# Four graph-attention layers over 128 graphs: rehearsed due times, layer 1's fold on another engine, and a repeat of rows without DRAM for two graphs

## The chip, the cores and the metric

The kernel runs on one core of one Trainium2 chip. The metric is the device time of one launch in microseconds, median over runs. A core has five engines, each with its own instruction stream executed in order: TensorE (PE; matmuls and transposes, with its weight loads shown as PEld), VectorE (DVE), ScalarE (ACT), GpSimd (POOL) and SyncE (SP, which here only issues DMA transfers). They wait for each other by semaphores. PE's results land in PSUM, eight banks of 128 x 512 floats.

## The reference

Input are 128 graphs of 128 nodes with 512 features each (float32), and an adjacency matrix per graph. For each graph four graph-attention layers follow each other, each adding to the residual stream `x`:

```
h = relu(layernorm(x))
layer 0: Wh = h @ W^T;  e = leaky_relu(Wh@a1 + (Wh@a2)^T), masked;  x += elu(softmax(e) @ h)
layer 1: xl = h @ W1 (512 -> 4 heads x 256); per head a score from xl.a_src and xl.a_dst,
         masked softmax over sources, out = attn^T @ xl, + bias, elu;
         then one head: gl = out @ W2 (1024 -> 512), same attention; x += result + bias
layer 2: scores from h.w_src and h.w_dst;  x += softmax(masked leaky_relu) @ h
layer 3: 8 heads x 64: Wh = h @ Wp; score from a 128-vector per head; x += relu(attn @ Wh)
```

A score of the form (h @ W) . a equals h . (W @ a), for layer 0 with W^T. The kernel uses this: products of the weights with the attention vectors ("folds") are made once, and stand as extra columns beside the weights (`w1x`, `w2x`, `wpx`) or as a row `u1`, `u2` on all partitions.

## The kernel before, in words

**Streams.** Each graph's work is a Python generator, `graph(b)`, that yields steps: one instruction, or a `Group` of up to four matmuls or transposes. It also yields requests: `Take` (a buffer of a tag with a fixed number of buffers), `Fork` (a second stream beside this one), `Join` (wait for that stream), `Until` (wait for a name, such as `"w1"`, to be reached). Ten graphs (`FLYING`) are in flight. When one ends, the next is started. Each graph forks the load of the graph two later (`AHEAD`).

**The order of issue.** `Scheduler.issue` builds the program once, at build time: among the next steps of all streams it takes the smallest (earliest start by estimated durations, rank, age). So the order within each engine's queue is fixed, and an instruction waits behind those that were put before it. `rank` of a graph's step is age x pace + due, where due comes from `plan`: the position of that step in the list of graph 0's steps, spread over the time of ten graphs. `plan` runs in `advance` when the first graph has ended. Until then `due` is None and all ranks are 0. Streams that aren't graphs (loads, the set-up, forks) always have rank 0.

**Set-up.** `setup()` is one stream of age 0.5. It issues the 4-byte-piece loads of `a1`, `a2`, `b1` on SP, then all weights in pieces of 512 KB to 1 MB on SP's queue, among them four attention vectors broadcast to all partitions (512 KB each for layer 1, 256 KB each for layer 2's), then two times four matmuls for `u1` and `u2` on PE; then `fold`, one DVE product-and-sum per column: 32 of 256 elements for layer 1's four heads, four row blocks and two vectors, then 16 of 512 for W2, then 16 DVE operations for Wp.

**The layers.** `norm_relu`: bn_stats and small steps on DVE and POOL, then h on ACT. `transposed`: PE transposes into a bank, ACT copies out. `projected`: matmul groups of four over the row blocks of a weight, ACT copies out. Layer 1 has 3 x 4 matmuls of 344 columns (w1x), 8 of 128 (et,xl), and 2 x 8 of 257 (w2x); layer 3 has 2 x 4 of 264 (wpx) and 8 of 65 (x,sd). In layers 0, 1 (its second half) and 2 the score row is repeated over the partitions by a PE transpose of a broadcast column (`attended`).

**`spread`** does the same for several rows: 4 rows of layer 1, 16 and later 8 of layer 3. One PE transpose, ACT writes `r`, SP writes `r` to DRAM (`d`), and SP reads it back broadcast to all partitions. Layer 1's spread and layer 3's second one are forks; layer 3's first one is part of the graph's stream. In layer 3 `sd` (1 MB, tag with 2 buffers) receives the 16 rows; DVE adds the mask, takes the maximum per row; the 8 rows of maxima are spread again; ACT applies Prelu and exp, PE multiplies (x,sd).

**Buffers that matter.** bank 8; `sd` 2; `x3` (layer 3's projection, filled from wpx and read by x,sd) 2; `ht` 3; `r4`, `r8`, `r16` 3 each; `junk` (the unused elementwise output of a dot) 2.

In the profile every graph instruction bears line L237, the call in `issue` (L245 in the changed kernel), so groups are told apart by their tiles: "bank<-w2x,y" is a matmul of weights `w2x` and `y` into a bank.

Of the kernel before, what the change touches and what calls it, by code (L numbers as in the profile page):

```python
# [22 lines left out]
AHEAD = 2  # L23

# [78 lines left out]
class Fork:  # L103


    def __init__(self, steps):
        self.steps = steps
# [21 lines left out]
class Scheduler:  # L129
    def __init__(self):  # L130
        self.streams = []
        self.engine_free = {}
        self.written = {}
        self.moved = 0.0
        self.taken = {}
        self.returned = {}
        self.tag_of = {}
        self.last_use = {}
        self.reached = set()
        self.done = []  # L140
        self.pace = 0.0
        self.due = None

    def give_back(self, *aps):
        for ap in aps:
            name = ap.tensor.name
            tag = self.tag_of.pop(name)
            self.taken[tag] -= 1
            heapq.heappush(self.returned[tag], self.last_use.get(name, 0.0))
# [7 lines left out]
    def advance(self, s):  # L157

        while True:
            want = s.next  # L160
            if want is None:
                try:
# [3 lines left out]
                    if s.like and self.due is None:  # L166
                        self.plan()
# [5 lines left out]
            if isinstance(want, Take):  # L173
                back = self.returned.setdefault(want.tag, [0.0] * want.bufs)
                if not back:
                    return
                self.taken[want.tag] = self.taken.get(want.tag, 0) + 1
                t = want.pool.tile(
                    want.shape, want.dtype, tag=want.tag, name=want.tag, bufs=want.bufs
                )  # L180
                self.tag_of[t.tensor.name] = want.tag
                self.written[t.tensor.name] = heapq.heappop(back)
                s.answer = t
            elif isinstance(want, Fork):
                s.answer = self.add(want.steps, s.age)
# [7 lines left out]
    def plan(self):  # L193

        load, length, self.due = {}, 0.0, []
        for step in self.done:
            self.due.append(length)
            load[step.engine] = load.get(step.engine, 0.0) + step.busy
            length += step.busy + step.delay
# [3 lines left out]
    def rank(self, s):  # L203
        if not s.like:
            return 0.0
        if not self.due:
            return 0.0
# [12 lines left out]
    def issue(self):  # L220
# [13 lines left out]
        if s.like and self.due is None and s.age == 0:  # L234
            self.done.append(step)
# [29 lines left out]
def kernel(  # L265
# [65 lines left out]
    nc.vector.tensor_scalar(off_diag, ident, -1.0, 1.0, ALU.mult, ALU.add)  # L331
    minus_half = const.tile([P, 1], F32, name="minus_half")
# [6 lines left out]
    w1x = const.tile([P, KC, E1 + HF], F32, name="w1x")  # L339
    w1 = w1x[:, :, E1:]  # L340
    w2x = const.tile([P, FC, E2 + D], F32, name="w2x")
    w2 = w2x[:, :, E2:]
    wpx = const.tile([P, KC, H3, E3 + K3], F32, name="wpx")
    wp = wpx[:, :, :, E3:]
# [10 lines left out]

    def on_all_partitions(t, row):
        return S.dma_start(out=t, in_=row.partition_broadcast(P))

    def fold(weight, vec, n, to):

        junk = yield tile_of("junk", 2, D)
        yield V.tensor_tensor_reduce(
            out=junk[:, :n],
            in0=weight,
            in1=vec,
            scale=1.0,
            scalar=0.0,
            op0=ALU.mult,  # L370
            op1=ALU.add,
            accum_out=to,
        )
        give_back(junk)

    def setup():
        acs = []
        for a in (l0_a1, l0_a2):
            acs.append(const.tile([P, KC], F32, name=f"ac{len(acs)}"))
            with nc.allow_non_contiguous_dma(reason="512 values, once"):  # L380
                nc.sync.dma_start(out=acs[-1], in_=a.rearrange("(c p) o -> p (c o)", p=P))
        with nc.allow_non_contiguous_dma(reason="1024 values, once"):
            nc.sync.dma_start(out=b1, in_=l1_b1.rearrange("(c p) -> p c", p=P))
# [3 lines left out]
        yield S.dma_start(out=w0, in_=l0_w.rearrange("(c p) f -> p c f", p=P))  # L387
        abs1 = []
        for a in (l1_src1, l1_dst1):
            ab = yield tile_of("y1", 2, FC, P)  # L390
            abs1.append(ab.rearrange("p c q -> p (c q)"))
            yield on_all_partitions(abs1[-1], a.rearrange("h f -> (h f)"))
        for c in range(0, KC, 2):
            yield S.dma_start(
                out=w1[:, c : c + 2, :],
                in_=l1_w1[c * P : (c + 2) * P].rearrange("(c p) f -> p c f", p=P),
            )
        abs2 = []
        for i, a in enumerate((l1_src2, l1_dst2)):
            abs2.append((yield tile_of("x2", 2, E2 + D))[:, :D])  # L400
            yield on_all_partitions(abs2[-1], a[0])
        for c in range(0, FC, 4):
            yield S.dma_start(
                out=w2[:, c : c + 4, :],
                in_=l1_w2[c * P : (c + 4) * P].rearrange("(c p) f -> p c f", p=P),
            )
        yield on_all_partitions(b2, l1_b2)
        yield on_all_partitions(w_src, l2_src)
        yield on_all_partitions(w_dst, l2_dst)
        yield on_all_partitions(b_l2, l2_b)  # L410
        yield S.dma_start(out=b_l3[:, 0], in_=l3_batt.partition_broadcast(P))
        wab = yield tile_of("sd", 2, 2 * H3, P)
        wa = wab.rearrange("p s q -> p (s q)")[:, : H3 * 2 * K3]
        yield on_all_partitions(wa, l3_watt.rearrange("h k -> (h k)"))
        wa = wa.rearrange("p (h k) -> p h k", h=H3)
        for c in range(KC):
            yield S.dma_start(
                out=wp[:, c], in_=l3_wp[c * P : (c + 1) * P].rearrange("p (h k) -> p h k", h=H3)
            )
        for ac, u in zip(acs, (u1, u2)):  # L420
            pu = yield bank()
            for c in range(KC):
                yield T.matmul(
                    pu,
                    lhsT=ac[:, c : c + 1].to_broadcast([P, P]),
# [4 lines left out]
            yield A.copy(u, pu)  # L430
            give_back(pu)
        give_back(w0)
        sched.reached.add("u")
        for c in range(KC):
            for s, ab in enumerate(abs1):
                for h in range(H1):
                    f = slice(h * F1, (h + 1) * F1)
                    to = w1x[:, c, s * H1 + h : s * H1 + h + 1]
                    yield from fold(w1[:, c, f], ab[:, f], F1, to)
        give_back(*abs1)  # L440
        sched.reached.add("w1")
        for c in range(FC):
            for s, ab in enumerate(abs2):
                yield from fold(w2[:, c, :], ab, D, w2x[:, c, s : s + 1])
        give_back(*abs2)
        sched.reached.add("w2")
        for c in range(KC):
            for s in range(2):
                prod = yield tile_of("junk", 2, D)
                p3 = prod.rearrange("p (h k) -> p h k", h=H3)  # L450
                yield V.tensor_tensor(p3, wp[:, c], wa[:, :, s * K3 : (s + 1) * K3], ALU.mult)

                yield V.tensor_reduce(wpx[:, c, :, 1 - s], p3, AX.X, ALU.add)
                give_back(prod)
        give_back(wab)
# [19 lines left out]
    def dot(h, vec, to):  # L475

        yield from fold(h, vec, D, to)

    def transposed(t, n, tag, bufs):

        r = yield tile_of(tag, bufs, n, P)
        pt = yield bank()
        yield Group(
            [T.transpose(pt[:, j * P : (j + 1) * P], t[:, j, :], ident) for j in range(n)]
# [5 lines left out]
    def spread(cols, n, to, func):  # L490


        r = yield Take(work, [n, P], f"r{n}", 3)
# [62 lines left out]
    def attended(own, other, mask, values, exact=False):  # L556
# [5 lines left out]
        et = yield from transposed(e, 1, "et0", 3)  # L562
# [6 lines left out]
    def projected(lhs, n_k, w, parts, to, beside=None):  # L569


        width = w.shape[2] // parts
        fork = None
        for i in range(parts):
            lo = i * width
            pm = yield bank()
            for g in range(0, n_k, 4):
# [5 lines left out]
                            rhs=w[:, c, lo : lo + width],  # L583
# [38 lines left out]
    def layer1(xt, mask):  # L622
        h = yield from norm_relu(xt)
        yield G.tensor_tensor(xt, xt, b2, ALU.add)
        ht = yield from transposed(h.rearrange("p (c q) -> p c q", q=P), KC, "ht", 3)
# [6 lines left out]
            ht, KC, w1x, 3, columns(fx, 3), lambda: spread(fx[:, :H1], H1, rows, AF.Copy)  # L632
# [6 lines left out]
        et = yield from transposed(e, H1, "et1", 3)  # L639
# [52 lines left out]
    def layer3(xt, mask, mask_t):  # L692
# [3 lines left out]
        ht = yield from transposed(h.rearrange("p (c q) -> p c q", q=P), KC, "ht", 3)  # L696
# [3 lines left out]
        fx = yield tile_of("x3", 2, H3, E3 + K3 + 1)  # L700
# [5 lines left out]
            wpx.rearrange("p c h k -> p c (h k)"),  # L706
# [7 lines left out]
        yield from spread(  # L714
            f.rearrange("p s h -> p (s h)"), 2 * H3, sd.rearrange("p s q -> p (s q)"), AF.Copy
        )
        d, e = sd[:, :H3], sd[:, H3:]
# [7 lines left out]
        fork = yield Fork(spread(mx, H3, d.rearrange("p h q -> p (h q)"), AF.Prelu))  # L725
# [44 lines left out]
    def load(b):  # L770

        if b % AG == 0:
# [4 lines left out]
        xs[b] = xpool.tile([P, D], F32, tag="xt", name="xt")  # L777
        yield S.dma_start(out=xs[b], in_=x[b])
# [7 lines left out]
    def graph(b):  # L786
        if b + AHEAD < B:
# [16 lines left out]
        yield from layer1(xt, m1)  # L804
# [7 lines left out]
        yield from layer3(xt, m3, m3t)  # L812
# [4 lines left out]
    with tc.manual_schedule():  # L817
        for i in range(min(AHEAD, B)):
            sched.add(load(i), i)
        flying = [sched.add(graph(0), 0, "graph")]  # L820
# [58 lines left out]
```

## Time and profile before

| | us |
|---|---|
| median of 3 runs | 3452.57 (3451.44 to 3454.29) |
| profiled execution | 3451.47 |
| its span, first to last instruction | 3449.7 |
| PE / DVE / ACT / POOL busy | 3362.5 / 2882.3 / 2379.8 / 1022.3 |
| w2x matmuls (4096 records, two to a matmul) | 975.0 busy |
| w1x matmuls (3072) | 953.5 |
| wpx matmuls (2048) | 499.6 |
| first matmul / first w1x / first w2x starts at | 11.83 / 43.64 / 78.53 |
| last h,et matmul (last graph, layer 2) starts at | 3391.58 |
| DMA moved, mean over the span | 94 GB/s |

How to read it: busy time is the sum over an engine's instructions. In the slices each digit is the busy share of a fortieth of the span (86 us) in tenths; PEclk is the clock granted to PE, in tenths of full. A line of the timeline gives the start (us from the span's start), the time covered, the engine, the line, the operation with its tiles, the size and the count, and in brackets the idle time before it and what ended it. A line of the view by stages gives the stretch, its length, the busy time of PE, PEld, DVE, ACT and POOL (instructions in brackets), the granted clock, the busy share of the DMA engines and GB/s. An idle stretch of an engine that isn't the bound costs nothing.

### The profile page before, as it was taken

What the parts mean: (1) busy time and instruction counts of PE and PEld (TensorE: products, weight loads), DVE (VectorE), ACT (ScalarE), POOL (GpSimd) and SP (SyncE); (2) the same over time, 40 slices, a digit from 0 to 9 for tenths busy, and PEclk for the clock granted to TensorE, in tenths of its full rate; (3) what the DMA queues carried; (4) which work ended last, traced back from release to release, by engine and by line L of the source; (5) the groups of instructions that cost most, each with busy time, mean ns of one, the idle gap of its engine ahead of it and who ended that gap; (6) DMA issues with size and microseconds to landing.
All of it is one profiled execution on the core that took longest, in us unless ns stands there. A gap on an engine that the chain in (4) does not pass through costs nothing.

```text
span 3449.7 us, 55292 instructions
## 1 busy us (share of the span) xinstructions
PE 3362.5 (97%) x16912; PEld 2619.4 (76%) x16912; DVE 2882.3 (84%) x9330; ACT 2379.8 (69%) x6659; POOL 1022.3 (30%) x1800
## 2 busy tenths in 40 slices
PE   5899999999999999999999999999999999999995
PEld 3677777777777777777777777777777777777774
DVE  7778888888888888888888888888888888888875
ACT  3567776777777777777777777777777777777763
POOL 2323233233233233233233233233233233233210
PEclk7999999999999999999999999999999999999996
DMA  4112222222222222222222222222222222222222
GB/s 159 38 56 102 98 85 102 98 87 102 97 86 102 96 90 102 94 89 102 93 92 101 92 91 101 92 95 100 91 93 99 92 96 99 90 95 99 84 89 99
DMA packets 126346, 325.00 MB, mean 94 GB/s; under 512 B 21088, under 2 KB 41056, under 8 KB 109664
## 3 DMA queue, kind: packets, MB, share of 16 engines
q1 hardware_dynamic: 126048, 321.46, 26.9%
q8 instruction: 134, 2.20, 0.3%
q14 instruction: 164, 1.34, 0.1%
HBM read 286.01 MB, written 35.39 MB: 93 GB/s over the span
## 4 chain that ended last, share of the span: by engine, by line
PE 96%; DVE 2%; ACT 1%; DMA 0%; issue 0%; POOL 0%; SPq 0%; POOLq 0%; ACTq 0%; DVEq 0%
PE bank L237 96%; DVE junk L237 1%; DVE sd L237 0%; ACT sd L237 0%; DVE t L237 0%; DMA sd<-in_L_gnn_W_dram 0%; DVE st L237 0%; DVE e L237 0%; ACT h L237 0%; DMA sd<-d 0%; DVE y L237 0%; DVE mx L237 0%; DVE m L237 0%; DVE xt L237 0%; ACT t L237 0%
## 5 line engine op out<-in xcount | busy, mean ns | idle before, releaser
L237 PE MATMUL bank<-w2x,y 128*128 128x257 f32 x4096 | 975.0, 380 | 0.1
L237 PE MATMUL bank<-w1x,ht 128*128 128x344 f32 x3072 | 953.5, 453 | 0.7 <-ACT ht L237 0.7
L237 PEld LDWEIGHTS bank<-w2x,y 128*128 128x128 f32 x4096 | 748.5, 190 | 140.5 <-issue 26.4
L237 PEld LDWEIGHTS bank<-w1x,ht 128*128 128x128 f32 x3072 | 564.5, 190 | 241.0 <-issue 2.6
L237 POOL TENSOR_SCALAR ve<-mv 128x1 f32<-128x1 f32 x512 | 137.1, 268 | 1584.5 <-DVE nm L237 806.0
L237 ACT ACTIVATE h<-xt,nmr,rstd 128x512 f32<-128x512 f32 x512 | 414.5, 810 | 208.1 <-DVE nmr L237 192.5
L237 PE MATMUL bank<-wpx,ht 128*128 128x264 f32 x2048 | 499.6, 387 | 0.0
L237 PEld LDWEIGHTS bank<-wpx,ht 128*128 128x128 f32 x2048 | 380.3, 191 | 95.3 <-issue 36.5
L237 ACT COPY et<-bank 128x128 f32<-128x128 f32 (+1 forms) x512 | 175.4, 344 | 321.0 <-PE bank L237 320.7
L237 ACT ACTIVATE e<-e,nm 128x128 f32<-128x128 f32 x896 | 354.3, 398 | 40.1 <-DVE nm L237 24.0
L237 ACT ACTIVATE sd<-sd,f 128x128 f32<-128x128 f32 x1024 | 364.2, 393 | 23.0 <-DVE sd L237 22.8
L237 DVE BATCH_NORM_STATS2 st<-xt 128x6 f32<-128x512 f32 x512 | 351.4, 686 | 1.5 <-DMA xt<-in_x_dram 1.5
L237 POOL TENSOR_TENSOR rstd<-ve,minus_half 128x1 f32<-128x1 f32 x512 | 291.5, 570 | 39.7
L237 PE MATMUL bank<-x,sd 128*128 128x65 f32 x2048 | 262.9, 273 | 14.8 <-ACT sd L237 14.8
L237 PEld LDWEIGHTS bank<-et,xl 128*128 128x128 f32 x2048 | 260.2, 192 | 20.7 <-ACT et L237 1.8
L237 PE MATMUL bank<-et,xl 128*128 128x128 f32 x2048 | 271.8, 276 | 0.9 <-ACT et L237 0.9
L237 DVE SCALAR_TENSOR_TENSOR xt<-bank,rz,xt 128x512 f32<-128x512 f32 x256 | 191.0, 746 | 96.9 <-PE bank L237 91.6
L237 PEld LDWEIGHTS bank<-x,sd 128*128 128x128 f32 x2048 | 254.6, 195 | 18.2 <-ACT sd L237 17.4
L237 DVE SCALAR_TENSOR_TENSOR nmr<-mv,rstd 128x1 f32<-128x1 f32 x512 | 139.9, 274 | 140.3 <-POOL rstd L237 138.3
L237 ACT COPY x<-bank 128x257 f32<-128x257 f32 (+1 forms) x512 | 191.1, 373 | 90.5 <-PE bank L237 82.9
L237 PE MATMUL bank<-h,et 128*128 128x512 f32 x512 | 249.1, 607 | 2.5 <-ACT et L237 2.5
L237 DVE CUSTOM_DVE_ANT_0 e<-bank,m 128x128 f32<-128x128 f32 x384 | 109.0, 284 | 148.2 <-PE bank L237 147.9
(86 smaller groups left out, 5752.1 us busy)
## 6 DMA issues: line engine op xcount, KB each, us to landing
sd<-d SPq DMA_DIRECT2D x128, 1024.0 KB
sd<-d SPq DMA_DIRECT2D x128, 512.0 KB
xt<-in_x_dram SPq DMA_DIRECT2D x128, 256.0 KB
e<-d SPq DMA_DIRECT2D x128, 256.0 KB
out_dram<-xt SPq DMA_DIRECT2D x128, 256.0 KB
at<-in_adj_dram SPq DMA_DIRECT2D x32, 256.0 KB
w1x<-in_L_gnn_W_dram SPq DMA_DIRECT2D x2, 1024.0 KB
w2x<-in_L_gnn_W_dram SPq DMA_DIRECT2D x2, 1024.0 KB
```

The costliest lines, as they stand in the source:

```text
L237: method(*args, **kw)
```

## The change

- `rehearse` runs the generator of graph 0 once before anything is issued, collecting its steps, and `plan` makes the due times from these. A stream that isn't a graph now has rank age x pace, and a `Fork` can be given an age.
- `setup()` loads in another order and in smaller pieces: W in four chunks first, then x of graph 0, then W1 in four chunks, two x loads, layer 2's vectors, W2 in eight chunks, and so on, the loads of graphs 0 to 11 among them. The 4-byte pieces (now also layer 1's attention vectors as columns) are issued on ACT's queue; the two 512-KB broadcast rows go. Weights lie in one tile per row block.
- The folds are forks with ages 0 (`fold_u`, `fold_w1`), 3 (`fold_w2`) and 6 (`fold_w3`). Layer 1's is done on PE: 32 transposes of W1's blocks, 8 ACT copies, 32 matmuls of two columns, 4 small ACT copies, for the 32 DVE dots. `fold_u` goes through W's chunks with both vectors at a time.
- The dots of all layers write their unused output to one tile `products`; the tags `r4`, `r8`, `r16` become one tag `r` with 4 buffers; `x3` has 3 buffers; layer 3's first spread is a fork too.
- For the last two graphs (`LATE`) `spread` does without DRAM: it transposes each column, broadcast, four to a bank, and ACT copies the bank out: 4, 16 and 8 transposes for three.

The diff, cut to its core:

```diff
+LATE = 2
...
-    def plan(self):
+    def rehearse(self, steps):
+        done, answer = [], None
+        try:
+            while True:
+                want = steps.send(answer)
+                answer = None
+                if isinstance(want, Step):
+                    done.append(want)
+                elif isinstance(want, Take):
+                    self.returned.setdefault(want.tag, [0.0] * want.bufs)
+                    answer, _ = self.take(want)
+        except StopIteration:
+            return done
+
+    def plan(self, steps):
 
         load, length, self.due = {}, 0.0, []
-        for step in self.done:
+        for step in steps:
...
     def rank(self, s):
         if not s.like:
-            return 0.0
-        if not self.due:
-            return 0.0
+            return s.age * self.pace
         due = self.due[s.index]
         return s.age * self.pace + due
...
+    w1x = rows_of("w1x", KC, E1 + HF)
+    w2x = rows_of("w2x", FC, E2 + D)
+    wpx = rows_of("wpx", KC, H3, E3 + K3)
...
+    def few(to, values):
+        with nc.allow_non_contiguous_dma(reason="at most 1024 values, once"):
+            nc.scalar.dma_start(out=to, in_=values)
 
     def setup():
+        for i, a in enumerate((l0_a1, l0_a2)):
+            few(a0[:, :, i], a.rearrange("(c p) o -> p (c o)", p=P))
+        for i, a in enumerate((l1_src1, l1_dst1)):
+            few(a1[:, :, i], a.rearrange("h (c p) -> p (h c)", p=P))
+        few(b1, l1_b1.rearrange("(c p) -> p c", p=P))
 
         w0 = yield tile_of("sd", 2, 2 * H3, P)
         w0 = w0.rearrange("p s q -> p (s q)").rearrange("p (c f) -> p c f", c=KC)
-        yield S.dma_start(out=w0, in_=l0_w.rearrange("(c p) f -> p c f", p=P))
-        abs1 = []
-        for a in (l1_src1, l1_dst1):
-            ab = yield tile_of("y1", 2, FC, P)
-            abs1.append(ab.rearrange("p c q -> p (c q)"))
-            yield on_all_partitions(abs1[-1], a.rearrange("h f -> (h f)"))
...
+        for c in range(KC):
+            yield S.dma_start(out=w0[:, c], in_=l0_w[c * P : (c + 1) * P])
+        yield Fork(fold_u(w0))
+        yield from load(0)
+        for c in range(KC):
+            yield S.dma_start(out=w1x[c][:, E1:], in_=l1_w1[c * P : (c + 1) * P])
+        yield Fork(fold_w1())
+        yield from load(1)
+        yield from load(2)
+        vecs = []
+        for row in (l1_src2, l1_dst2):
+            vecs.append((yield tile_of("x2", 2, E2 + D))[:, :D])
+            yield S.dma_start(out=vecs[-1], in_=row[0].partition_broadcast(P))
+        for c in range(FC):
+            yield S.dma_start(out=w2x[c][:, E2:], in_=l1_w2[c * P : (c + 1) * P])
+        yield Fork(fold_w2(vecs), 3)
...
+        yield Fork(fold_w3(wa), 6)
+        for b in range(6, min(FLYING + AHEAD, B)):
+            yield from load(b)
...
+    def fold(blocks, vecs, per, to):
+        k = vecs.shape[2]
+        pf = yield bank()
+        for g in range(0, len(blocks), 4):
+            wt = yield from transposed(blocks[g : g + 4], "ht", 3)
+            yield Group(
+                [
+                    T.matmul(
+                        pf[:, j // per * k : (j // per + 1) * k],
+                        lhsT=wt[:, j - g, :],
+                        rhs=vecs[:, j, :],
...
+                    )
+                    for j in range(g, g + 4)
+                ]
+            )
+            give_back(wt)
+        n = len(blocks) // per * k
+        yield A.copy(to, pf[:, :n].rearrange("p (a b) -> p a b", b=to.shape[2]))
+        give_back(pf)
+
+    def fold_w1():
+        for w in w1x:
+            to = w[:, :E1].rearrange("p (s h) -> p h s", h=H1)
+            yield from fold(blocks_of(w[:, E1:]), a1, F1 // P, to)
         sched.reached.add("w1")
...
-    def spread(cols, n, to, func):
-        r = yield Take(work, [n, P], f"r{n}", 3)
+    def spread(cols, n, to, func, late):
+        if late:
+            for g in range(0, n, 4):
+                pt = yield bank()
+                yield Group(
+                    [
+                        T.transpose(
+                            pt[:, j * P : (j + 1) * P],
+                            cols[:, g + j : g + j + 1].to_broadcast([P, P]),
+                            ident,
+                        )
+                        for j in range(4)
+                    ]
+                )
+                yield A.activation(
+                    out=to[:, g * P : (g + 4) * P], in_=pt, func=func, alpha=SLOPE
+                )
+                give_back(pt)
+            return
+        r = yield Take(work, [2 * H3, P], "r", 4)
+        r = r[:n]
...
-        fx = yield tile_of("x3", 2, H3, E3 + K3 + 1)
+        fx = yield tile_of("x3", 3, H3, E3 + K3 + 1)
...
-        yield from spread(
-            f.rearrange("p s h -> p (s h)"), 2 * H3, sd.rearrange("p s q -> p (s q)"), AF.Copy
+        fork = yield Fork(
+            spread(
+                f.rearrange("p s h -> p (s h)"),
+                2 * H3,
+                sd.rearrange("p s q -> p (s q)"),
+                AF.Copy,
+                late,
+            )
         )
+        yield Join(fork)
...
-        if b + AHEAD < B:
+        if FLYING + AHEAD <= b + AHEAD < B:
             yield Fork(load(b + AHEAD))
...
-        yield from layer1(xt, m1)
+        yield from layer1(xt, m1, b >= B - LATE)
...
-        for i in range(min(AHEAD, B)):
-            sched.add(load(i), i)
-        flying = [sched.add(graph(0), 0, "graph")]
-        setting_up = sched.add(setup(), 0.5)
-        started = 1
+        sched.rehearse(load(0))
+        sched.plan(sched.rehearse(graph(0)))
+        sched.reached.clear()
+        sched.add(setup(), 0)
+        flying, started = [], 0
```

## The prediction

> **What bounds the kernel now.** I read the page first: busy time and slices.
>
> ```profile
> span 3449.7 us, 55292 instructions
> ...
> PE 3362.5 (97%) x16912; PEld 2619.4 (76%) x16912; DVE 2882.3 (84%) x9330; ACT 2379.8 (69%) x6659; POOL 1022.3 (30%) x1800
> ...
> PE   5899999999999999999999999999999999999995
> ...
> PEclk7999999999999999999999999999999999999996
> ```
>
> TensorE is the bound; what it loses lies in the first two slices and the last. The busy time by stage (columns: us, then PE, PEld, DVE, ACT, POOL busy, granted clock, DMA share, GB/s) sharpens that.
>
> ```profile
> 50.00:75.00 25.00, 17.34 (x63) 11.31 (x62) 23.34 (x87) 8.86 (x27) 5.46 (x7) 0.81 0.08 22
> 140.00:165.00 25.00, 20.33 (x79) 12.41 (x77) 24.11 (x85) 16.45 (x49) 13.35 (x18) 0.86 0.12 43
> 400.00:3200.00 2800.00, 2800.00 (x14268) 2194.38 (x14268) 2396.89 (x7791) 2008.85 (x5625) 861.44 (x1513) 1.00 0.28 95
> 3392.00:3450.00 58.00, 25.52 (x107) 20.41 (x106) 25.19 (x41) 16.95 (x44) 2.34 (x6) 0.59 0.25 95
> ```
>
> From 400 to 3200 PE never waits at full clock. Around 50 to 75 and 140 to 165 DVE is 93 to 96% busy and PE waits for it. In the last 58 us everything waits in turn.
>
> From the starts of successive PE groups in the timeline between 1000 and 3000 I took the spacing of each group: four w1x matmuls 2.31 us, four w2x 1.74, four wpx 1.78, four et,xl 0.89, four x,sd (65 columns) 0.84, h,et 0.86, four transposes 0.44. A graph comes to 25.9 us, 128 graphs to 3314 us; the span's other 136 us are the two ends. I call "lag" the time at an instruction minus the graph work that PE has issued by then. The PE timeline of the head:
>
> ```profile
> 11.83 9.95 PE L237 MATMUL bank<-sd,ac 128*128 128x512 f32 x16 [11.83 <-DMA sd<-in_L_gnn_W_dram]
> ...
> 43.64 9.52 PE L237 MATMUL bank<-w1x,ht 128*128 128x344 f32 x24
> ...
> 78.53 5.56 PE L237 MATMUL bank<-w2x,y 128*128 128x257 f32 x16
> ...
> 210.83 0.27 PE L237 MATMUL bank<-ident,xl 128*4 128x128 f32 x1 [0.47 <-ACT xl L237]
> ```
>
> At 78.53 the work done is 21.2 us: lag 57.3. At 210.83 it is 132.1: lag 78.7, and after that it stays (3142 us hold 121.3 graphs). The tail:
>
> ```profile
> 3391.58 2.07 PE L237 MATMUL bank<-h,et 128*128 128x512 f32 x2 [0.36 <-ACT et L237]
> ...
> 3404.09 3.68 PE L237 MATMUL bank<-x,sd 128*128 128x65 f32 x16 [4.42 <-ACT sd L237]
> 3407.56 5.19 PE L237 MATMUL bank<-wpx,ht 128*128 128x264 f32 x16
> ...
> 3414.47 3.78 PE L237 MATMUL bank<-wpx,ht 128*128 128x264 f32 x16
> ...
> 3434.21 3.68 PE L237 MATMUL bank<-x,sd 128*128 128x65 f32 x16 [4.96 <-ACT sd L237]
> ...
> 3441.56 3.67 PE L237 MATMUL bank<-x,sd 128*128 128x65 f32 x16 [3.68 <-ACT sd L237]
> ```
>
> From 3353 on, 41.4 us of work take 96.6: 55 lost. The last wpx (its ht was ready by 3400) waits for x3, whose two buffers the x,sd before it free. Then the DRAM repeat, in the SP and DVE timeline of the last graph:
>
> ```profile
> 3419.63 0.32 SPq L237 DMA_DIRECT2D d<-r  x1
> ...
> 3421.26 0.33 SPq L237 DMA_DIRECT2D sd<-d  x1
> ...
> 3425.98 1.22 DVE L237 TENSOR_TENSOR sd<-sd,m 128x1024 f32<-128x1024 f32 x1 [1.06 <-DMA sd<-d]
> ```
>
> 6.35 us for 16 rows; the 8 rows of the maxima follow the same way.
>
> **What the Trainium skill says.** "TensorE: Matmul & The Clock Gate", Part 1: PE falls to half rate after an idle window of about 3.4 us and needs about as much activity to come back. The trace agrees in kind: PEclk is 0.5 from 24 to 48, 65 to 82 and nearly throughout after 3390, and PE warms 5.7 us after its start at 11.83. The same page, Part 4: a transpose does not count as activity for the gate; no run here shows it, but it speaks for cold transposes in the tail. "Perfetto Trace Analysis", Identifying the Most-Contended Engine, warns that matmul busy percentage misleads; hence the stage table and the waits, which agree: no PE wait in 400 to 3200.
>
> **The change, part by part.** *Head: loads and u.* w0 now comes in four chunks, first on its queue; the 4-byte loads move to ACT's queue (five issues, about 0.5 us each, nothing of ACT waits behind them yet). Issue at 0.74, plus the 3.5 us from issue to landing that the first x load shows: about 4.3. Both u's follow in 16 half matmuls, cold for 5.7 us: done near 14.5, first dot near 15 (before: 19.0 for u1, 22.4 for u2). The two 512-KB broadcast loads of layer 1's vectors go.
>
> *Head: fold of layer 1.* 32 DVE dots at 0.345 = 11.0 us leave DVE, the engine that is full there. PE gets 32 transposes x 0.109 = 3.5 and 32 two-column matmuls: at the 65-column row's 0.21 each 6.9, sum 10.4 (at the floor of about 25 ns between short matmuls that "TensorE: Matmul & The Clock Gate", Back-to-back issue gap, states: 0.8, sum 4.3, an estimate). ACT gets 8 copies at 0.47 and 4 small ones, about 5 us, while it is under half busy. PE is idle then, so this is inside the wait for DVE, except where it precedes a graph's step in order.
>
> *Head: due times.* Before, all graphs had rank 0 until graph 0 ended at 164; now graph 0 goes first. In the new issue order DVE's instructions from the first dot to graph 0's y (input of its w2x) sum to 47.7 us: 28 dots x 0.61, 14 add-max x 0.21, 10 bn_stats x 0.604, 39 small x 0.085, 23 of 128 columns x 0.19, 13 tensor ops of 512 x 0.63, 4 x 0.6, 5 x 0.335, one 0.604, one 1.135. So w2x can't start before 15 + 47.7 = 62.7, and with some 5 us that DVE waits for PE and ACT, 68. PE has 28.4 us of graph work ahead of it in that order: lag 34.5 to 40, against 57.3. Afterwards I cumulated DVE and PE sums along each order. Before, DVE stood up to 31 us ahead of PE's work and was still 24 ahead at PE work 105. After, it is 8 ahead at work 46, level at 81 and 16 behind at 134: layer 3 (8.2 us DVE against 5.7 PE per graph) first comes at work 96, before at 58, and layers 0 to 2 need 14.3 DVE for 20.2 PE. So little more should be lost: lag at the end of the head 47 (39 to 65), against 78.7: **-31.7** (-40 to -14). The folds of w2 (16 dots, 9.7) and w3 (16 ops, about 9.5) stay on DVE, only later.
>
> *Tail.* The third x3 buffer lets graph 126's wpx move ahead of the last h,et: PE does 4.2 us more by then (3.55 + 0.65). From the last h,et to the end the new order gives, PE warm / cold: to the h transposes 6.75 (as before), ht copied 1.7; wpx 3.6 / 5.2 with f 1.0; 16 transposes and the last ACT copy 2.5 / 4.2; DVE mask 1.14 and max 1.13, and graph 126's 1.13 in the same queue; 8 transposes with Prelu 2 x 0.59 behind eight 0.29 ones 3.5 / 3.9; difference 1.13, exp 1.0, x,sd 1.74 / 3.7, end 1.3, output DMA 3.0. Sum 30.6 / 37; graph 126's 16 transposes and copies, graph 125's x,sd and 126's mask stand in front of these in the same queues: 6.4 / 12. Together 37 to 49, I take 43, before 58.1: -15.1 + 4.2 = **-10.9** (-17 to -5). It adds 50 transposes, 5.4 us of PE, inside these sums; without the wait they would cost that.
>
> *Steady state.* The six DMAs of a graph's three repeats stay as they are. `products` for junk, one tag r (4 buffers, three spreads in 26 us, each held some 5 us) and the forked first spread put no wait where DVE and ACT are ahead: nothing, while PE covers it; uncovered, an r reuse would hold ACT's queue, and ht and et behind it. But the new order repeats over two graphs and some links have less PE work in between: e1's transposes to et,xl 8.8 to 3.7 us, h's transposes to wpx 11.0 to 2.9, e0's to x,et 6.4 to 2.6; x,sd gets more (16.8 to 17.4 or 19.3). The tightest stretch of ACT, 23 instructions, sums to 7.65 us and leaves about 1.5; before, a gap of 1.73 passes without a wait. **0** (bounds -0 and +0.5 us per graph, +59).
>
> Sum: -31.7 - 10.9 = -42.6 on the profiled span, 3449.7 to 3407. The profiled execution's time is 3451.5, 1.8 above its span; the median of runs 3452.6, 2.9 above: **3410**.
>
> **Rivals.** *A, as worked: 3410 (3398 to 3424).* *B, more:* DVE's gaps vanish (lag 39, -40) and the tail stays warm (-15 to -17): 3396. For it: 11 us of dots gone from the full engine. Against: PE is cold in every wait. *C, the head gives half back:* cold PE and in-order waits (a w1 block's matmul queued behind a fold's transpose whose weights land late) keep the lag near 62, or layer 3's DVE work still starves PE: -17 and -8, 3428. For it: clock 0.81 to 0.86 in those stages. *E, it does not do what it says:* due times don't matter as the data's arrival sets the head, the tail is bound by DVE and ACT anyway: within 7 us. Against: DVE, not DMA (share 0.08), is full at 50 to 75. *D, the other side:* the tighter links make PE wait each graph in the steady stage, for ACT's et or ht copy behind a Prelu or exp that itself waits for DVE. With a loss of δ over 118 graphs it eats the 42.6 from δ = 0.36 us on; at 0.4 us: +47, 3457; at 0.5, 3469. For it: 2.9 against 11.0 us of cover, DVE 86% and ACT 72% busy. Against: 2.9 is still above the smallest gap that works.
>
> **How the numbers follow.** Chances: A 0.55, B 0.12, C 0.19, E 0.04, D 0.10. Forecast 3410, the likeliest. Leaving out D and E and the upper end of C, and the lower end of B: 3393 to 3438. About 0.2% (7 us) is what a measurement of this kernel tells from no change: faster 0.86, same 0.04, slower 0.10.
>
> **What would show it.** First dot by 15 to 16; w1x without DVE dots before it; w2x of graph 0 near 68 (before 78.5); lag near 47 at 210; no PE wait in 400 to 3200 (if there is, for et or ht from ACT, D holds); wpx of the last two graphs right after their ht, no DRAM repeat after 3370, last h,et to the end 37 to 49 us. Wrong if w2x comes after 75, if the lag grows beyond 60 by 210 through layer 3 on DVE, or if the steady stage loses PE time.

## The result, and the profile after

The changed kernel takes 3515.1 us (median of 5 runs, 3512.43 to 3516.45) against 3452.16 before: ratio 1.0181, 95% interval 1.0166 to 1.0196. It is 1.8% slower; the forecast was 3410, and the range 3393 to 3438 doesn't hold it. Of the rivals, D came true in kind: PE waits once per graph in the steady stage. But it waits for another engine than D named.

The page of the changed kernel (span; busy time; PE's slices and its clock; the chain that ended last, by engine):

```profile
span 3513.3 us, 56160 instructions
...
PE 3403.0 (97%) x17058; PEld 2652.5 (75%) x17058; DVE 2986.9 (85%) x9266; ACT 2311.3 (66%) x6679; POOL 1092.2 (31%) x1800
...
PE   8999999999999999999999999999999999999997
...
PEclk8999999999999999999999999999999999999998
...
PE 56%; DVE 24%; ACT 10%; POOL 7%; issue 2%; DMA 0%; ACTq 0%; POOLq 0%
```

The chain in the kernel before:

```profile
PE 96%; DVE 2%; ACT 1%; DMA 0%; issue 0%; POOL 0%; SPq 0%; POOLq 0%; ACTq 0%; DVEq 0%
```

The slices look better than before: the first starts at 8, the last ends at 7. They can't show what was lost, since a 9 stands for 90% and more. The chain shows it: PE's share fell from 96% to 56%, and POOL has 7% of it, where it had none. The busy time by stage (us, then PE, PEld, DVE, ACT, POOL busy, granted clock, DMA share, GB/s):

```profile
50.00:75.00 25.00, 18.11 (x72) 10.91 (x71) 23.33 (x84) 14.51 (x44) 11.42 (x15) 0.93 0.07 21
140.00:165.00 25.00, 24.49 (x121) 18.96 (x120) 15.45 (x50) 16.58 (x44) 9.28 (x14) 1.00 0.14 54
400.00:3200.00 2800.00, 2741.46 (x13834) 2142.68 (x13833) 2426.31 (x7549) 1877.23 (x5455) 894.05 (x1467) 1.00 0.26 92
3450.00:3513.00 63.00, 38.59 (x180) 31.79 (x179) 35.84 (x69) 27.49 (x65) 4.31 (x13) 0.73 0.14 55
```

From 140 to 165 PE is now busy 24.5 of 25 us (20.3 before). But from 400 to 3200 it did 13834 matmul records where it had done 14268, and DVE is busy for longer with fewer instructions. PE's waits in that stage (who waited, for whom; us in all, times, longest) have one line; before there was none:

```profile
PE bank L245 <- POOL f L245: 58.5, 105, 0.7
```

`f` is the small POOL sum of layer 3's score columns; its transpose on PE is the first step of the repeat of 16 rows. Here is one such wait in the timeline of the changed kernel (start us, us, engine, operation, idle before and what ended it):

```profile
1002.14 1.27 POOL L245 TENSOR_TENSOR xt<-xt,t 128x512 f32<-128x512 f32 x1 [0.70 <-DVE t L245]
...
1002.66 1.02 PE L245 MATMUL bank<-h,et 128*128 128x512 f32 x2
...
1002.92 0.36 ACT L245 COPY x<-bank 128x264 f32<-128x264 f32 x1
...
1003.50 1.19 DVE L245 TENSOR_TENSOR sd<-sd 128x1024 f32<-128x1024 f32 x1
...
1003.52 1.05 PE L245 MATMUL bank<-et,xl 128*128 128x128 f32 x8
1003.67 1.10 POOL L245 TENSOR_SCALAR ve<-mv 128x1 f32<-128x1 f32 x1 [0.26 <-DVE mv L245]
...
1004.73 0.22 POOL L245 TENSOR_TENSOR f<-x,b_l 128x16 f32<-128x16 f32 x1
...
1005.01 0.28 PE L245 MATMUL bank<-ident,f 128*16 128x128 f32 x1 [0.43 <-POOL f L245]
```

wpx ends at 1002.66 and its copy at 1003.28. f's input is there then, but POOL has `ve` (a small sum of another graph's layernorm) ahead of it, which waits for its own input and then takes 1.10 us instead of 0.22: it ends 0.08 us after DVE's 128x1024 difference does. PE has only h,et and et,xl in between (1.75 us at the rounded spacings) and stands at the transpose. In the next graph f stands behind the POOL sum into xt, and is itself held:

```profile
1029.80 1.92 DVE L245 TENSOR_TENSOR sd<-sd 128x1024 f32<-128x1024 f32 x1
...
1030.59 1.21 POOL L245 TENSOR_TENSOR f<-x,b_l 128x16 f32<-128x16 f32 x1
...
1031.86 0.28 PE L245 MATMUL bank<-ident,f 128*16 128x128 f32 x1 [0.68 <-POOL f L245]
```

In the kernel before, the second copy of wpx, f and its transpose lay so:

```profile
1001.42 0.38 ACT L237 COPY x<-bank 128x264 f32<-128x264 f32 x1
...
1002.40 0.22 POOL L237 TENSOR_TENSOR f<-x,b_l 128x16 f32<-128x16 f32 x1
...
1007.01 0.27 PE L237 MATMUL bank<-ident,f 128*16 128x128 f32 x1
```

f was ready 4.4 us before PE came to it. In the changed kernel the two patterns alternate: of the 75 graphs from 1000 to 3000 f follows a held `ve` in 38 and is held itself in 37. In the order of issue the PE work between the end of wpx and the transpose of f is 5.73 us before and 1.73 us after, the same in every graph of the steady stage.

**Where the time went.** I counted the trace's matmul records, each at the steady spacing that the prediction took (transposes at 0.1093 us each), and call the time that is not graph work lost (the fold's 3.5 and the late transposes' 5.45 us count as lost too). All kernels, in us from the start of the profiled span:

| kernel | to 211 | 211 to 3200 | 3200 to the end | sum lost | median |
|---|---|---|---|---|---|
| before | 78.3 | 1.2 | 55.6 | 135.1 | 3452.2 |
| changed | 53.5 | 92.8 | 52.5 | 198.8 | 3515.1 |
| e1 in the stream | 52.6 | 0.0 | 45.8 | 98.4 | 3414.8 |
| e2 before, forked | 75.9 | 70.1 | 60.5 | 206.5 | 3524.0 |
| e3 f priced | 52.7 | 0.7 | 50.4 | 103.8 | 3420.5 |
| e4 halves | 54.1 | 74.8 | 49.7 | 178.6 | 3494.9 |
| e5 e1, LATE 0 | 53.4 | 0.2 | 47.7 | 101.3 | 3416.7 |
| e6 e1, fold on DVE | 55.0 | 0.4 | 44.8 | 100.2 | 3416.9 |
| e7 e1, late due | 61.6 | 0.8 | 46.5 | 109.0 | 3423.1 |
| e8 xt on DVE | 55.7 | 64.4 | 52.7 | 172.8 | 3487.0 |
| e9 e1, two x3 | 51.9 | 0.6 | 51.7 | 104.3 | 3420.4 |
| e10 e1, two x3, LATE 0 | 53.6 | 1.1 | 55.6 | 110.3 | 3426.7 |
| e11 before, three x3 | 78.0 | 0.4 | 49.0 | 127.4 | 3443.1 |
| e12 e1, ages 0 | 57.8 | 0.5 | 46.7 | 105.0 | 3420.2 |

Head and tail gain 24.8 and 3.1 us (the tail's last waits for f, from 3200 to 3450, included), the steady stage loses 91.6: the sum is the 63.6 us by which the span grew. The lags at 211 and the tail's losses that the expectations of e5 to e7 and e12 name were counted on a clock that starts 11 us before the span, so they are some 10 us too high at 211 and too low at the end; the differences that these expectations argue from are hardly touched by it.

### The profile page after: what moved, and what is told of

Its sections match the earlier page's. It is cut to its first block, busy times and chain, and to the rows that moved or that the text cites. A ratio compares the mean times of both kernels' runs of the same rounds, so it can differ in the third digit from the quotient of the medians.

```text
span 3513.3 us, 56160 instructions
## 1 busy us (share of the span) xinstructions
PE 3403.0 (97%) x17058; PEld 2652.5 (75%) x17058; DVE 2986.9 (85%) x9266; ACT 2311.3 (66%) x6679; POOL 1092.2 (31%) x1800
## 4 chain that ended last, share of the span: by engine, by line
PE 56%; DVE 24%; ACT 10%; POOL 7%; issue 2%; DMA 0%; ACTq 0%; POOLq 0%
PE bank L245 56%; DVE sd L245 5%; DVE t L245 4%; ACT e L245 3%; DVE xt L245 3%; DVE products L245 3%; DVE y L245 2%; POOL f L245 2%; POOL xt L245 2%; DVE mx L245 2%; POOL ve L245 2%; DVE e L245 2%; ACT sd L245 2%; ACT h L245 2%; DVE st L245 1%
## 5 line engine op out<-in xcount | busy, mean ns | idle before, releaser
L245 ACT ACTIVATE sd<-sd,f 128x128 f32<-128x128 f32 x1024 | 399.3, 393 | 242.2 <-DVE sd L245 242.2
L245 POOL TENSOR_SCALAR ve<-mv 128x1 f32<-128x1 f32 x512 | 200.4, 392 | 1120.8 <-DVE mv L245 992.3
L245 PEld LDWEIGHTS bank<-wpx,ht 128*128 128x128 f32 x2048 | 370.9, 191 | 58.8 <-ACT ht L245 2.5
L245 PEld LDWEIGHTS bank<-et,xl 128*128 128x128 f32 x2048 | 267.8, 191 | 121.3 <-issue 89.4
L245 POOL TENSOR_TENSOR rstd<-ve,minus_half 128x1 f32<-128x1 f32 x512 | 315.6, 617 | 37.1
L245 DVE CUSTOM_DVE_ANT_0 products<-h,u 128x512 f32<-128x512 f32 x256 | 177.0, 691 | 138.3 <-ACT h L245 130.8
L245 POOL TENSOR_SCALAR m<-m 128x128 f32<-128x128 f32 x128 | 71.5, 558 | 701.8 <-DVE m L245 694.6
L245 PE MATMUL bank<-h,et 128*128 128x512 f32 x512 | 264.7, 599 | 0.1
L245 ACT ACTIVATE t<-t 128x1024 f32<-128x1024 f32 x128 | 135.3, 1057 | 166.9 <-DVE t L245 166.8
L245 ACT ACTIVATE sd<-sd 128x1024 f32<-128x1024 f32 x128 | 135.4, 1058 | 155.2 <-DVE sd L245 155.1
```

The lines of the kernel that those rows point to most:

```text
L245: method(*args, **kw)
```

## The experiments

**e1 and e2: the fork, undone and alone.** The changed kernel makes layer 3's first repeat a fork. A fork's rank is age x pace with no due time, while the same step in the graph's stream has the due time of a late step added. When two steps could start equally early, the planner takes the smaller rank. So it puts the fork's transpose ahead of the younger graphs' work as soon as it believes f to be ready. e1 takes the fork back. (A late graph has more steps than graph 0, so the index into the due times is capped.)

```diff
-        fork = yield Fork(spread(f..., late))
-        yield Join(fork)
+        yield from spread(f..., late)
...
-        due = self.due[s.index]
+        due = self.due[min(s.index, len(self.due) - 1)]
```

> The changed kernel with layer 3's first repeat (16 rows) back in the graph's own stream, with its own due time, instead of a fork. The order of issue then has 5.73 us of PE work between the end of wpx and the transpose of f, as before, against 1.73 in the changed kernel. Theory T (the fork alone draws that transpose too near to POOL's f): PE's wait for f in 400 to 3200 (58.5 us in the changed kernel) is gone, the lag grows by less than 6 us from 211 to 3353 (97 in the changed kernel), time 3410 to 3425. Rival R (the new due times and load order make a steady order in which DVE and POOL hold each other up whatever the fork): the wait moves to another instruction, 3480 or more.

3414.8 us, ratio 0.9891 (0.9876 to 0.9906). The stage from 400 to 3200:

```profile
400.00:3200.00 2800.00, 2800.00 (x14270) 2203.55 (x14270) 2429.22 (x7792) 1988.11 (x5627) 859.13 (x1514) 1.00 0.28 95
```

PE doesn't wait at all, and all other edits of the changed kernel stay. e2 does the reverse in the kernel before, where a fork has rank 0:

```diff
-        yield from spread(f..., AF.Copy)
+        fork = yield Fork(spread(f..., AF.Copy))
+        yield Join(fork)
```

> The kernel before, with one edit: layer 3's first repeat is a fork. The gap in PE work between wpx and the transpose of f falls from 5.73 to 1.73 us. T: PE waits for POOL's f in every graph, 0.5 to 0.8 us, time 3510 to 3550. R: 3445 to 3460, the fork does nothing by itself.

3524.0 us, ratio 1.0206 (1.0191 to 1.0222), and one wait of PE in the same stage:

```profile
PE bank L237 <- POOL f L237: 41.6, 79, 0.6
```

The fork alone costs 71 us, with old due times, old loads and old folds. T holds both ways, R falls. A wait in every graph had been expected; it is 79 of 106. And f itself runs at its usual length here (mean 236 ns): in the graphs that wait it stands behind a `ve` that is held.

**e3: the fork kept, f priced later.** The planner believed POOL's f to land 0.1 us after its end.

```diff
-        yield G.tensor_tensor(f, fx[:, :, :E3]..., b_l3, ALU.add)
+        step = G.tensor_tensor(f, fx[:, :, :E3]..., b_l3, ALU.add)
+        step.delay = 3.0
+        yield step
```

> The changed kernel, fork kept, but the planner is told that POOL's f lands 3 us after its end (0.1 before). The order of issue then has 4.75 us of PE work between wpx and the transpose of f. T: as in stream, 3410 to 3430. A rival F (a fork's rank, age x pace without a due time, disturbs the order in other places too): 3470 or more in spite of the gap.

3420.5 us (0.9904, 0.9889 to 0.9919), no wait of PE from 400 to 3200. So the fork's harm goes when this distance is given back, and its rank disturbs nothing else that costs time there (F falls).

**e4 and e8: why f is late, with the order of issue kept.** Two causes stand in the timelines above: POOL held during DVE's difference (X), and f behind the 1.27-us sum into xt on POOL (Q). e4 halves the difference, e8 takes the sum off POOL; both keep the old prices, so that the planner issues in the same order.

```diff
# e4
-        yield V.tensor_tensor(e, e, d, ALU.subtract)
+        cut = H3 // 2
+        halves = [V.tensor_tensor(e[:, i : i + cut], e[:, i : i + cut], d[:, i : i + cut], ALU.subtract)
+                  for i in (0, cut)]
+        step = Group(halves)
+        step.busy = V.tensor_tensor(e, e, d, ALU.subtract).busy
+        yield step
# e8
+    GV = Engine("POOL", nc.vector)
...
-        yield G.tensor_tensor(xt, xt, t, ALU.add)
+        yield GV.tensor_tensor(xt, xt, t, ALU.add)
```

> The changed kernel with the difference of layer 3 (128x1024 on DVE) in two halves of 512, priced as one, so that the order of issue on all engines is the same. If a POOL instruction is held as long as a DVE instruction of this kind runs (X), f and the ve ahead of it are held 0.6 us instead of 1.1: the loss per graph falls from 0.82 to 0.2 to 0.5 us, 3440 to 3480. If POOL's f is late by POOL's own queue alone (Q): 3510 to 3520.

> The changed kernel with layer 0's sum into xt (1.27 us on POOL, ahead of f) issued on DVE at the same place, priced as before, so that the order of issue is the same but for the queue of this instruction. If f is late because it stands behind that sum on POOL (Q) as well as because POOL is held during DVE's difference (X): loss per graph from 0.82 to 0.1 to 0.4 us, 3435 to 3465. If X alone counts: 0.6 to 0.8, 3490 to 3510.

e4: 3494.9 us (1.0122, 1.0105 to 1.0139). e8: 3487.0 (1.0104, 1.0089 to 1.0119). e4 lies between the values expected, too slow for the larger effect and much too fast for none. e8 is far too slow for both causes, and 3 us under the range for X alone. So the times don't separate the two; the groups and the starts do. POOL's group of f (busy us, mean ns, idle before) in the kernel before:

```profile
L237 POOL TENSOR_TENSOR f<-x,b_l 128x16 f32<-128x16 f32 x128 | 28.8, 225 | 86.8 <-ACT x L237 86.8
```

in the changed kernel:

```profile
L245 POOL TENSOR_TENSOR f<-x,b_l 128x16 f32<-128x16 f32 x128 | 86.1, 673 | 23.8 <-ACT x L245 23.8
```

and in e8:

```profile
L245 POOL TENSOR_TENSOR f<-x,b_l 128x16 f32<-128x16 f32 x128 | 49.8, 389 | 114.1 <-ACT x L245 114.1
```

Counting each start of a matmul against the spacing of the one before it, from 400 to 3200: in the changed kernel the transpose of f starts late 105 times, by 76.0 us in all. In e4 that is 42.0 us, in e8 25.5 us in only every second graph (in the others f starts 0.1 us after its copy). So both causes are real. But the gain is partly given back, since the next tight link shows up, the transpose of layer 1's score columns (xl), a fork too. PE's waits in e4:

```profile
PE bank L245 <- POOL f L245: 18.0, 60, 0.3
PE bank L245 <- ACT xl L245: 8.9, 52, 0.2
```

and in e8:

```profile
PE bank L245 <- POOL f L245: 16.8, 53, 0.3
PE bank L245 <- ACT xl L245: 15.8, 52, 0.3
```

By starts, xl loses 17.7 us in e4 and 24.8 in e8, where in the changed kernel it lost nothing. The expectations had priced the one link alone. How X and Q share the loss exactly stays open; the distance of 1.73 us is the common cause that e1 and e3 remove. Another 11 us of the changed kernel's loss from 400 to 3200 are no wait: twice per graph a w1x or w2x group follows x,sd directly there and loses 0.055 us. Only the four kernels with the distance of 1.73 us have these neighbours; in the others a transpose follows x,sd.

**e5, e9, e10, e11: the tail.** e5 sets LATE = 0 in e1, e9 gives e1 two x3 buffers, e10 does both, e11 gives the kernel before three.

```diff
# e5, e10
-LATE = 2
+LATE = 0
# e9, e10
-        fx = yield tile_of("x3", 3, H3, E3 + K3 + 1)
+        fx = yield tile_of("x3", 2, H3, E3 + K3 + 1)
# e11, on the kernel before
-        fx = yield tile_of("x3", 2, H3, E3 + K3 + 1)
+        fx = yield tile_of("x3", 3, H3, E3 + K3 + 1)
```

> The kernel of e1 (3414.8) with LATE = 0: the last two graphs repeat their rows through DRAM like the others; x3 keeps three buffers. The tail after 3353 lost 44.8 us in the kernel before and 32.6 in e1. If the repeat on TensorE carries the tail's gain: 8 to 13 us more than e1, 3423 to 3428. If the third x3 buffer carries it: 3413 to 3418.

> The kernel of e1 (3414.8) with two x3 buffers instead of three; rows of the last two graphs still on TensorE. If the third buffer carries the tail's gain (e5 left it in and lost only 2 us): the last wpx waits for an earlier graph's x,sd again, 5 to 11 us more, 3419 to 3426. If it doesn't: 3413 to 3418, and the tail's gain comes from the order that the early due times make.

> The kernel of e1 with both tail edits undone: two x3 buffers, LATE = 0. If each covers for the other (either one is enough): 8 to 13 us more than e1, 3423 to 3428, while e5 and e9 lose little. If x3 alone carries it: as e9. If neither does: 3413 to 3419.

> The kernel before with three x3 buffers, nothing else. If the third buffer shortens the tail by itself: 4 to 11 us less, 3441 to 3448. If the order of issue hides it: 3449 to 3455.

e5: 3416.7 us (runs from 3414.4 to 3417.6, e1's from 3414.6 to 3416.7: no difference that these runs can tell). e9: 3420.4 (3420.1 to 3422.9). e10: 3426.7 (3424.3 to 3427.9). e11: 3443.1 against 3451.8 for the kernel before beside it, ratio 0.9975 (0.9965 to 0.9985). (The kernel before itself differs by up to 1.3 us, 3451.4 to 3452.7, from one set of runs to another, so smaller differences between experiments say nothing.) The third buffer carries most of the tail: 5.6 us in e9, 8.7 alone in e11. In e9 the wpx of the last graph but one is again queued behind an x,sd that frees its buffer:

```profile
3380.11 3.68 PE L245 MATMUL bank<-x,sd 128*128 128x65 f32 x16 [4.42 <-ACT sd L245]
3383.59 5.26 PE L245 MATMUL bank<-wpx,ht 128*128 128x264 f32 x16
```

The repeat on TensorE is worth some 6 us where the wpx come late (e10 against e9) and nothing that can be measured where the third buffer has let them come early (e5 against e1): the round trip through DRAM is then presumably hidden by the other late graph's work, which no run separates. That they cover for each other holds in part, since e9 already loses 5.6 of e10's 11.9 us.

**e6, e7, e12: the head.** e6 folds layer 1 by DVE dots from broadcast rows again, e7 keeps all ranks 0 until graph 0 has ended (and those of loads, folds and forks for the whole run), e12 gives the folds of W2 and Wp age 0; each on e1.

```diff
# e6
-        yield Fork(fold_w1())
+        yield Fork(fold_w1(rows1))
...
         for w in w1x:
-            to = w[:, :E1].rearrange("p (s h) -> p h s", h=H1)
-            yield from fold(blocks_of(w[:, E1:]), a1, F1 // P, to)
+            for s, row in enumerate(rows1):
+                for h in range(H1):
+                    f = slice(h * F1, (h + 1) * F1)
+                    to = w[:, s * H1 + h : s * H1 + h + 1]
+                    yield from dot(w[:, E1:][:, f], row[:, f], to)
# e7
+        sched.known, sched.due = sched.due, None
...
-        if not s.like:
-            return s.age * self.pace
+        if not s.like or not self.due:
+            return 0.0
...
+                    if s.like and self.due is None:
+                        self.due = self.known
# e12
-        yield Fork(fold_w2(vecs), 3)
+        yield Fork(fold_w2(vecs))
-        yield Fork(fold_w3(wa), 6)
+        yield Fork(fold_w3(wa))
```

> The kernel of e1 with layer 1's fold as 32 DVE dots again and its two vectors as broadcast rows of 512 KB, loaded ahead of W1. If the fold's move carries the head: 11.0 us of DVE work come back where DVE is full and the loads come first again, lag at 211 from 59.6 to 70 to 76, time 3425 to 3432. If the early due times carry it: lag 59 to 63, 3414 to 3419.

> The kernel of e1 with all ranks 0 until graph 0 has ended, as before; loads and folds as in the changed kernel. If the early due times carry the head: graph 0 reaches w2x later, lag at 211 from 59.6 to 70 to 80, 3425 to 3436. If loads and folds carry it: lag 58 to 63, 3413 to 3419.

> The kernel of e1 with the folds of W2 and Wp at age 0 instead of 3 and 6, that is as urgent as graph 0. If putting these DVE operations (about 19 us) off is what the head gains beside the due times and layer 1's fold: lag at 211 from 59.6 to 64 to 72, 3419 to 3427. If it isn't (the load order and the earlier u carry the rest): 58 to 62, 3413 to 3418.

e6: 3416.9 (3416.5 to 3417.7), head 55.0 against e1's 52.6. e7: 3423.1 (3421.7 to 3425.3), head 61.6. e12: 3420.2 (3414.9 to 3421.3, which overlaps with e1: unclear by time; head 57.8). So the ranks, early due times above all, are the largest part of the head's 25 us that was taken apart, about 9; as e7 changes the ranks of loads and folds too, it can't be told how much of it is the due times alone. The fold on TensorE gives hardly 3, and there the larger effect named as possible, 10 us or more, did not come. The rest (load order, earlier u) was not tried alone, and the parts need not add up. The PE timeline of the changed kernel says what became of the fold:

```profile
4.52 10.48 PE L245 MATMUL bank<-sd,a 128*128 128x512 f32 x16 [4.52 <-DMA a<-in_L_gnn_a_dram]
14.84 0.60 PE L245 MATMUL bank<-ident,w1x 128*128 128x128 f32 x4
16.16 1.05 PE L245 MATMUL bank<-a,ht 128*128 128x2 f32 x8 [0.73 <-ACT ht L245]
...
27.28 1.06 PE L245 MATMUL bank<-ident,w1x 128*128 128x128 f32 x4
29.07 1.87 PE L245 MATMUL bank<-a,ht 128*128 128x2 f32 x8 [0.52 <-ACT ht L245]
...
41.35 1.09 PE L245 MATMUL bank<-a,ht 128*128 128x2 f32 x8
42.44 2.48 PE L245 MATMUL bank<-w1x,ht 128*128 128x344 f32 x8
```

Eight rounds of transposes, ACT copy and short matmuls follow each other from 14.84 to 42.4, mostly at half clock (four transposes take 0.60 at first, 1.06 later), seven of them with a wait for ACT. The sum of their own times was 10.4 us, but as a chain, with a few other steps of the first graphs in between, they last 27.6, and the first w1x starts at 42.44 (43.64 before; 38.13 in e6).

e1 is faster than both kernels, by 1.1% over the one before.

## Why the prediction was wrong

**The failing step is the steady state.** It put the forked first spread at nothing "where DVE and ACT are ahead", and looked at the distances of other links (ht to wpx, et to et,xl, e0 to x,et, and mx to x,sd). The link from wpx by ACT's copy and POOL's f to the transpose of f was not among them. It is the one link of a steady graph that the change turns into a fork, and it went from 5.73 to 1.73 us. POOL, 30% busy, doesn't occur in that argument as an engine that PE waits for. Its queue and its holds by DVE decide nevertheless: f's mean went from 225 to 673 ns, and where f keeps its length (e2), the `ve` ahead of it doesn't.

The threshold was right: rival D had to cost 0.36 us per graph to eat the gain, and the loss is 0.83 (86.6 us from 400 to 3200, over the 105 graphs that pass in it). Its place was wrong: ACT's et and ht copies, whose links had shrunk most (11.0 to 2.9 and 8.8 to 3.7 us), never made PE wait. The argument "2.9 is above the smallest gap that works" held for them; for f 1.73 was as large as that smallest gap, and too small, since what runs within it is two engines and a queue and not one copy. A chance of 0.10 for D, and a range that left it out, were too sure for an order of issue that repeats differently.

**The head** was forecast at -31.7 and came to -24.8. First dot by 15: 14.80. But w2x of graph 0 was to start near 68 and started at 78.96, which the prediction itself had named as a sign against it. The DVE work of 47.7 us to graph 0's y took 63.6 (14.80 to 78.4). DVE waited for ACT, PE and POOL some 9 us in it (5 forecast), and a few instructions took longer than in e1's steady stage, about 5 us in all (a mask of 0.21 took 1.29 while POOL's sum into xt ran). By w2x the lag is 50.4 against 57.0, a gain of 7 where 17 to 23 were forecast. The rest of the gain comes after it: from there to 211 the lag of the kernel before grew by another 21 us, that of the changed one by 3, where the forecast had let it grow from about 37 to 47. So the head's sum lies in the stated bounds partly by luck, as two terms were off in opposite ways. The fold's own 10.4 us was a sum where a chain counted.

**The tail** was forecast at -10.9. In e1, where the waits for f don't reach into it, it is 55.6 to 45.8: -9.8. From the last h,et to the end 37 to 49 us were given: 45.4 in the changed kernel, 40.6 in e1. The step "third x3 buffer" was right and carries most of it; the repeat on TensorE adds nothing measurable to it. (The prediction's cold terms add up to 36.3 and not 37, which changes nothing.)

**The starting point** was right: the prediction gave the head a lag of 78.7 and the tail 55; counted by records they are 78.5 at 210.83 and 55.5 after 3353.

Without the wait, A's range (3398 to 3424) holds e1's 3414.8: A's sum held, within its bounds, for everything but the one link.

## What to carry to other kernels

When a planner writes the order of issue, a change of a step's rank is a change of its distance to what it needs: after any such edit, list for every instruction of the bounding engine the work between it and its producer, along each engine in between, small ones included, and compare it with the old list. An engine that is 30% busy can stall the bound if its queue holds a long instruction, or if another engine holds it. A step of several hops through other engines costs its chain and not its sum when nothing else fills the hops; and before building a faster path for a tail, add a buffer, which was one character here and worth 8.7 us alone.

## What the runs showed of the hardware

In these traces POOL and DVE hold each other up for as long as one instruction of the other runs. While DVE's 128x1024 difference of two SBUF tensors runs (1.21 us alone), POOL's 128x1 `ve` takes 1.10 instead of 0.22 and the 128x16 f up to 1.22; while POOL's 128x512 sum runs (1.27), the same difference takes up to 1.93, `sd<-sd,m` 2.02 (1.22 in the kernel before), and in the steady stage a mask of 0.21 up to 0.93. DVE instructions with one operand in PSUM, bn_stats and the 128x1024 reduce kept their times (0.68 for `y<-bank,b` and bn_stats, 1.22 for the reduce) beside POOL. The Trainium skill says so in "SBUF — State Buffer", section "Who interferes with whom": a DVE instruction with two SBUF inputs contends with a GpSimd instruction that reads SBUF, and the loser waits for the whole instruction. The trace agrees for the difference and `sd<-sd,m`; the mask, with one SBUF input, is not a case of that sentence. e4 agrees too, as with the difference in halves f takes 0.63 us in mean and 0.69 at most. In e1 and e3, whose order keeps f and `ve` away from the difference, these take 0.22 again and the difference 1.21; there POOL's 128x512 sum into xt takes longer instead, 1.73 us in every graph of the steady stage against 1.27 in the changed kernel.
